# Layer 0's softmax sums taken in 32-column blocks beside the attention heads' sums, and both reciprocals spread over the partitions through DRAM

## The chip, the core and the metric

The kernel runs on one core of a Trainium2 chip. The core has a matrix engine (TensorE, PE in the profile; PEld is its weight load), a vector engine (VectorE, DVE), an activation engine (ScalarE, ACT), a general engine (GpSimd, POOL) and SyncE (SP), which in this kernel only issues DMAs. Each engine works through its own list of instructions in order, and semaphores tie the lists together. The metric is the device time of one execution in microseconds (us), the median of several runs.

## The reference

A graph attention layer and then a masked multi-head attention layer, each with a layer norm and a ReLU ahead of it and a residual sum behind it. `x` is 64 x 256 x 512 in fp32, `adj` is a 256 x 256 mask that all 64 batches share.

```python
# layer 0
h = jnp.maximum(_layernorm(x), 0.0)
Wh = h @ W
logits = leaky_relu((Wh @ a_src)[:, :, None] + (Wh @ a_dst)[:, None, :])     # slope 0.2
attn = softmax(where(adj == 0, -inf, logits), axis=-1)
x = x + attn @ Wh
# layer 1: 8 heads of 64
h = jnp.maximum(_layernorm(x), 0.0)
q, k, v = split_heads(h @ Wq.T + bq), split_heads(h @ Wk.T + bk), split_heads(h @ Wv.T + bv)
attn = softmax(where(adj == 0, -inf, q @ k.T / 8), axis=-1)
x = x + merge_heads(attn @ v) @ Wo.T + bo
```

Two softmax sums are concerned here: in layer 0 one number for each of the 256 nodes of a batch, in layer 1 one for each node and head.

## The kernel before

A group is one batch (`GB = 1`), so there are `G = 64` groups of 256 tokens, in two tiles of 128 partitions. Everything is fp32. Projections and the layer-0 aggregation use a scheme of seven products of half-size blocks instead of eight (`products`, L170, with the sums that it needs made on POOL by `combine`, L163, and the results added up on DVE).

All work is software-pipelined by hand. Each stage is a generator; `first_half` and `second_half` (L1025 to L1031) list, for iteration `i`, which stage makes its next step and for which group: for instance `O` is `(output, -2)`, `E0` is `(weights0, 2)`, `A_OLD` is `(attention, -1)`, `Q0` is `(quarters0, 2)`, `U0` is `(aggregate0, 2)`, `V` is `(project_v, 0)`. The order of these lists is the order of the instructions on every engine. All tiles in PSUM come from one pool of 8 banks (`bank`, L139). Most work tiles in SBUF have a single buffer.

The steps that matter:

- **Layer-0 weights** (`weights0`, L518). ACT makes two exponentials, DVE takes their maximum (L537), POOL applies the mask (L540, `em`) and adds the two halves of the sources (L542, `esum`, 128 x 256). The sum over the 128 partitions is a matmul with a square of ones (L556): its result, `ps`, holds the sum for each of the 256 targets, the same in all 128 partitions. DVE clamps it from below (L558) and takes the reciprocal (L559); the tile is called `rb0` in the code and `rb` in the profile, which leaves numbers out. This is the third step of `E0`, at the end of `first_half`.
- **Layer-0 operands** (`quarters0`, L566), for groups from `PLAIN = 3` on. POOL makes four block sums of `h` (L165 to L168, `hq`), multiplies `em` by the reciprocals (L578), and makes four block differences of it (L588, `eq`). `aggregate0` (L595) then has PE form the seven products (L606, `pu`), which DVE adds up.
- **Head sums** (`head_sums`, L873), inside the last step of `attention`. The sums of a head over the 128 source partitions are taken with a 128 x 32 stationary operand `half`: for each `e` of 4 pairs of heads, the result goes to PSUM partitions 32e to 32e+31, 16 equal rows for each head of the pair (L878, `psm`). DVE takes the reciprocal of that 128 x 256 tile (L886, `rc`).
- **Spreading them** (L905 to L915). To scale the attention output, the reciprocals of a head are needed on all 64 partitions that hold its values. SyncE issues eight DMAs, one per head, each from one row of `rc` to 64 partitions of `rb`. `scale` (L932) multiplies by `rb` on DVE (L936).
- **What follows on POOL.** After `eq`, POOL computes the inverse standard deviations of two layer norms (L474 to L476), on which ACT's normalisations L504 (`h`) and L729 (`xn`) wait; PE transposes `xn` at L750.

For the last two groups the reciprocals are spread by a matmul with `pick` (L922) instead.

Of the kernel before, what the change touches and what calls it, by code (L numbers as in the profile page):

```python
# [9 lines left out]
F32 = mybir.dt.float32  # L10
# [6 lines left out]
P = 128  # L17
# [6 lines left out]
Q = 32  # L24
# [4 lines left out]
def kernel(  # L29
# [26 lines left out]
    nc = tc.nc  # L56
    B, N, D = x.shape
    NC = N // P
    DC = D // P
    NT = GB * NC  # L60
    TOK = NT * P
    G = B // GB
    DH = D // HEADS
# [5 lines left out]
    dram = ctx.enter_context(tc.tile_pool(name="dram", bufs=1, space=bass.MemoryType.DRAM))  # L69
# [12 lines left out]
    ones = const.tile([P, P], F32, tag="ones", name="ones")  # L82
# [49 lines left out]
    def bounded():  # L132
        weights = ctx_b.enter_context(tc.tile_pool(name="weights", bufs=1))
        big = ctx_b.enter_context(tc.tile_pool(name="big", bufs=1))
        work = ctx_b.enter_context(tc.tile_pool(name="work", bufs=1))
# [3 lines left out]
        def bank(shape, name):  # L139
            return ps_mm.tile(shape, F32, tag="mm", name=name)  # L140
# [207 lines left out]
        pick = weights.tile([P, P], F32, tag="pick", name="pick")  # L348
# [10 lines left out]
        def constants():  # L359

            ok = weights.tile([P, 2 * DC + 5], F32, tag="ok", name="ok")
            rows = weights.tile([P, 2 * DC], F32, tag="rows", name="rows")
            gms = []
            for n in range(2):
                w_q = whole((wq_sb, wk_sb)[n])  # L370

                gm = work.tile([P, DC, DH], F32, tag="gram", name=f"gram_{n}", bufs=2)
                gms.append(gm)
                for pair in range(2):
                    pg = bank([P, 2, DH], f"pgram_{n}_{pair}")
                    for e in range(2):
                        for c in range(DC):
                            for r in range(2):
                                at = e * P + r * DH
                                wc = w_q[c // 2][pair][:, c % 2, at : at + DH]  # L380
                                nc.tensor.matmul(
                                    pg[r * DH : (r + 1) * DH, e, :], wc, wc,
                                    start=(c == 0), stop=(c == DC - 1),
                                )
                    yield
                    nc.vector.tensor_copy(gm[:, 2 * pair : 2 * pair + 2, :], pg)
                    yield
            for n, gm in enumerate(gms):
                pgs = [bank([P, DC, DH], f"pgram2_{n}_{r}") for r in range(2)]
                for e in range(DC):  # L390
                    for r in range(2):
                        half_p = slice(r * DH, (r + 1) * DH)
                        part = gm[half_p, e, :]
                        nc.tensor.matmul(pgs[r][half_p, e, :], part, part, start=True, stop=True)
                yield
                for e in range(DC):
                    for r in range(2):
                        half_p = slice(r * DH, (r + 1) * DH)
                        ab = work.tile([P, DH], F32, tag="gabs", name=f"gabs_{n}_{e}_{r}")
                        nc.scalar.activation(  # L400
                            ab[half_p], pgs[r][half_p, e, :], AF.Abs,
                            accum_out=rows[half_p, n * DC + e : n * DC + e + 1],
                        )
                yield
            for _ in range(10):
                yield
            sq = weights.tile([P, 4], F32, tag="sq", name="sq")
            for j, col in enumerate((cols["bq"], cols["bk"])):
                junk = work.tile([P, DC], F32, tag="e2", name=f"junk_c_{j}")
                nc.vector.scalar_tensor_tensor(  # L410
                    junk, col, 1.0, col, op0=ALU.mult, op1=ALU.mult, accum_out=sq[:, j : j + 1]
                )
            for _ in range(4):
                yield
            pq = bank([P, 2], "pq")
            nc.tensor.matmul(pq, ones, sq[:, 0:2], start=True, stop=True)
            yield
            nc.vector.tensor_scalar(
                ok[:, 2 * DC + 2 : 2 * DC + 4], pq, 1.0, None, op0=ALU.is_le
            )  # L420
            yield
            for j in range(2):
                junk = work.tile([P, D], F32, tag="e2", name=f"junk_w_{j}")
                nc.vector.scalar_tensor_tensor(
                    junk, wa[j], 1.0, wa[j], op0=ALU.mult, op1=ALU.mult, accum_out=sq[:, 2 + j : 3 + j]
                )
                yield
            nc.vector.tensor_scalar(ok[:, 0 : 2 * DC], rows, 1.0, None, op0=ALU.is_le)
            nc.vector.tensor_scalar(ok[:, 2 * DC : 2 * DC + 2], sq[:, 2:4], 1.95, None, op0=ALU.is_le)
            yield  # L430
            big_v = weights.tile([P, 1], F32, tag="big_v", name="big_v")
            nc.vector.tensor_reduce(big_v, svs, AX.X, ALU.add)
            nc.vector.tensor_scalar(
                ok[:, 2 * DC + 4 : 2 * DC + 5], big_v, 1.0e6, None, op0=ALU.is_le
            )
            okm = weights.tile([P, 1], F32, tag="okm", name="okm")
            nc.vector.tensor_reduce(okm, ok, AX.X, ALU.min)
            for _ in range(12):
                yield
            pk = bank([1, 1], "pok")  # L440
            nc.tensor.matmul(pk, okm, ones[:, 0:1], start=True, stop=True)
            nc.vector.tensor_scalar(flag, pk, P - 0.5, None, op0=ALU.is_lt)
            yield
            picks()
            yield

        class Stats:

# [30 lines left out]
        nodes, edges, sums0, lefts, norms, qkv, vs, outs = {}, {}, {}, {}, {}, {}, {}, {}  # L479
# [38 lines left out]
        def weights0(g):  # L518
# [22 lines left out]
            esum = work.tile([P, N], F32, tag="esum", name=f"esum_{g}")  # L541
            engine.tensor_tensor(esum, em[:, 0, :], em[:, 1, :], op=ALU.add)  # L542
            edges[g] = [em]
            yield

            if g == 0:
                ps = bank([P, NT], f"ps_{g}")
                for t in range(NT):
                    nc.tensor.matmul(
                        ps[:, t : t + 1], esum[:, t * P : (t + 1) * P], ones[:, 0:1],  # L550
                        start=True, stop=True,
# [7 lines left out]
            nc.vector.reciprocal(rs, rs)  # L559
            edges[g].append(rs)  # L560
            yield


        PLAIN = 3

        def quarters0(g):  # L566

# [257 lines left out]
        def attention(g):  # L825
# [46 lines left out]

            def head_sums():  # L873

                psm = bank([P, N], f"psm_{g}")
                for r in range(2):
                    for e in range(DC):
                        nc.tensor.matmul(  # L878
                            psm[e * Q : (e + 1) * Q, :],
                            half[:, r, :],  # L880
                            sums[e][:, r, :],
                            start=(r == 0),
                            stop=(r == 1),
                        )
                rc = work.tile([P, N], F32, tag="rc", name=f"rc_{g}")
                nc.vector.reciprocal(rc, psm)  # L886
                return rc

            exs = [scores(e) for e in range(DC)]
# [4 lines left out]
            if g == G - 1:  # L894
# [3 lines left out]
                rc = head_sums()  # L898
                values(1, exs[2:4])
            else:  # L900
                for j in range(2):
                    values(j, exs[2 * j : 2 * j + 2])
                rc = head_sums()
            if g < G - 2:
                rb = work.tile([P, DC, N], F32, tag="rb", name=f"rb_{g}")  # L905
                for e in range(DC):
                    for r in range(2):
                        src = rc[e * Q + r * (Q // 2) : e * Q + r * (Q // 2) + 1, :]
                        nc.sync.dma_start(
                            rb[r * DH : (r + 1) * DH, e, :],  # L910
                            bass.AP(
                                tensor=src.tensor, offset=src.offset,
                                ap=[src.ap[0], [0, DH], [1, N]],
                            ),
                        )  # L915
            else:

                yield
                rb = [bank([P, N], f"prb_{g}_{e}") for e in range(DC)]
                for e in range(DC):  # L920
                    rows = slice(e * Q, (e + 1) * Q)
                    nc.tensor.matmul(rb[e], pick[rows, :], rc[rows, :], start=True, stop=True)  # L922
            outs[g] = aT, rb
            yield

# [89 lines left out]
        def aside(n=1):  # L1015
# [3 lines left out]
        K, V, W, O = (project_qk, 0), (project_v, 0), (transform0, 1), (output, -2)  # L1019
        N0, D0, E0, U0 = (normalize0, 3), (normalize0, 2), (weights0, 2), (aggregate0, 2)  # L1020
        Q0 = (quarters0, 2)
# [1 line left out]
        A, A_OLD, BO = (attention, 0), (attention, -1), (bias_rows, 0)  # L1023
        AS, AS_OLD = (scale, -1), (scale, -2)
        first_half = [  # L1025
            (load, 3), O, D0, K, AS_OLD, O, K, O, K, E0, O, K, E0, O, US, A_OLD, K, O, K, BO, O, K, E0,
        ]
        second_half = [
            A_OLD, A, Q0, A, W, N0, W, W, V, N0, W, W, W, N1, W, N1, A, V, V, V, A, N0, N1, U0, V, AS,
            U0, X1, V, X1, V, X1,  # L1030
        ]  # L1031

# [259 lines left out]
```

## Time and profile before

| | |
|---|---|
| time, median of 3 (range) | 2847.4 us (2846.96 to 2849.59) |
| span of the profiled execution | 2845.2 us |
| granted TensorE clock | full speed |
| sum over the partitions for layer 0, L556 | 126 records of 379 ns (median), two for each of 63 matmuls |
| clamp L558, reciprocal L559 (128 x 256) | 411 ns, 1753 ns, 63 of each |
| the same two on 128 x 2 (group 0) | 159 ns, 166 ns |
| head sums L878 | 1024 records of 379 ns; weight load 110 ns |
| reciprocal L886 | 1758 ns, 64 of them |
| broadcast DMAs L909 | 496 of 64 KB, 4.9 us from issue to landing |
| DMA queue q1 | 82470 packets, 107.53 MB, 23.7% of 16 engines |

A duration of a matmul record is that of a pipelined instruction and overlaps the next one's, so what PE spends is read from the starts of successive groups and not from the durations. A "record" is one pass group of an fp32 matmul: each matmul shows two. Lines such as `[1.58 <-PE psm L878]` give the idle time of the engine before the instruction and what ended it.

### The profile page before, as it was taken

To read this page: it belongs to the slowest core of one execution; us is meant where nothing else is said; L and a number is where in the kernel's file an instruction comes from. 1 tells how busy PE (TensorE), PEld (TensorE's weight loads), DVE (VectorE), ACT (ScalarE), POOL (GpSimd) and SP (SyncE) were. 2 spreads that over 40 slices of the span, in tenths; PEclk is the share of its full clock that TensorE was granted. 3 is DMA by queue.
4 is the path that set the end of the run, shared out by engine and by line. 5 is a ranking of instruction groups with operands and counts; after the bars stand their busy time and mean duration, and the time that the engine had idled before them with its cause. 6 is when DMAs were issued, how large, how long until landed. Compare 5 with 4: busy or idle time off the path is not lost. (4 is left out here: it accounts for less than half of the span.)

```text
span 2845.2 us, 53317 instructions
## 1 busy us (share of the span) xinstructions
PE 2828.9 (99%) x20316; PEld 2472.3 (87%) x20316; DVE 2473.5 (87%) x3946; ACT 1257.3 (44%) x3045; POOL 1607.0 (56%) x2016
## 2 busy tenths in 40 slices
PE   9999999999999999999999999999999999999998
PEld 6888988988889889888898898888988988889886
DVE  7998988888889888888898888888988888889875
ACT  5444444443444444434444444344454443444532
POOL 2656556566565565665655655656556556565541
PEclk9999999999999999999999999999999999999999
DMA  4122122221221222212212222122122221221221
GB/s 134 23 38 38 34 42 33 36 45 31 38 38 34 42 33 36 45 31 38 39 33 42 33 36 46 31 38 40 32 42 33 36 45 31 38 42 30 34 42 27
DMA packets 82826, 111.01 MB, mean 39 GB/s; under 512 B 11524, under 2 KB 48644, under 8 KB 82566
## 3 DMA queue, kind: packets, MB, share of 16 engines
q1 hardware_dynamic: 82470, 107.53, 23.7%
q8 instruction: 164, 2.69, 0.4%
q14 instruction: 96, 0.79, 0.1%
q0 software_dynamic: 96, 0.01, 0.0%
HBM read 41.43 MB, written 33.55 MB: 26 GB/s over the span
## 5 line engine op out<-in xcount | busy, mean ns | idle before, releaser
L701 DVE TENSOR_TENSOR x<-po,x 128x1024 f32<-128x1024 f32 x875 | 593.8, 685 | 130.2 <-PE po L207 122.9
L851 DVE TENSOR_TENSOR ex<-ex,maskT 128x512 f32<-128x512 f32 x512 | 435.3, 890 | 0.0
L474 POOL TENSOR_SCALAR ve<-ssq 128x2 f32<-128x2 f32 x127 | 25.1, 198 | 483.8 <-ACT h L463 250.6
L846 ACT ACTIVATE ex<-psc 128x512 f32<-128x512 f32 x512 | 257.7, 627 | 89.5 <-PE psc L838 89.4
L871 ACT COPY aT<-pav 128x512 f32<-128x512 f32 x128 | 74.9, 585 | 499.2 <-PE pav L863 468.1
L511 DVE SCALAR_TENSOR_TENSOR junk<-wa,h 128x512 f32<-128x512 f32 x252 | 276.6, 1098 | 7.9 <-ACT h L504 1.1
L216 PEld LDWEIGHTS pqk<-hs,wq_sb 128*128 128x128 f32 x2016 | 264.4, 192 | 12.9
L216 PE MATMUL pqk<-hs,wk_sb 128*128 128x128 f32 x2016 | 266.3, 275 | 0.0
L216 PE MATMUL pqk<-hs,wq_sb 128*128 128x128 f32 x2016 | 265.8, 275 | 0.0
L207 PE MATMUL pv<-wv_sb,hs 128*128 128x256 f32 x1024 | 262.9, 380 | 0.6 <-DVE v L194 0.5
L540 POOL TENSOR_TENSOR em<-e,maskT 128x512 f32<-128x512 f32 x62 | 79.6, 1283 | 321.7 <-DVE e L537 312.0
L207 PE MATMUL po<-wo_sb,as 128*128 128x256 f32 x992 | 255.2, 380 | 0.0
L207 PE MATMUL po<-w_sb,us 128*128 128x256 f32 x1008 | 248.5, 379 | 0.0
L216 PEld LDWEIGHTS pqk<-hs,wk_sb 128*128 128x128 f32 x2016 | 245.4, 192 | 0.0
L838 PE MATMUL psc<-qk 64*128 64x256 f32 x2048 | 239.0, 383 | 0.3 <-DVE rc L886 0.3
L863 PE MATMUL pav<-ex,v 128*64 128x256 f32 x2048 | 235.4, 382 | 0.0
L838 PEld LDWEIGHTS psc<-qk 64*128 64x128 f32 x2048 | 193.1, 187 | 46.9 <-issue 25.0
L165 POOL TENSOR_TENSOR hs<-hT 128x256 f32<-128x256 f32 x64 | 47.0, 735 | 319.2 <-PE pv L207 319.2
L853 DVE TENSOR_TENSOR sm<-ex 128x512 f32<-128x512 f32 x256 | 210.5, 822 | 8.9
L863 PEld LDWEIGHTS pav<-ex,v 128*64 128x64 f32 x2048 | 141.2, 137 | 85.8 <-issue 20.3
L207 PEld LDWEIGHTS po<-w_sb,us 128*128 128x128 f32 x1008 | 191.4, 190 | 26.3 <-DVE x L701 0.3
L216 PEld LDWEIGHTS pqk<-hT,wq_sb 128*128 128x128 f32 x1512 | 198.2, 192 | 9.6
(211 smaller groups left out, 6564.5 us busy)
## 6 DMA issues: line engine op xcount, KB each, us to landing
x<-in_x_dram SPq DMA_DIRECT2D x64, 512.0 KB, 5.6
out_dram<-x SPq DMA_DIRECT2D x128, 256.0 KB, 2.0
rb<-rc SPq DMA_DIRECT2D x496, 64.0 KB, 4.9
wq_sb<-in_L_gnn_Wq_dram SPq DMA_DIRECT2D x4, 256.0 KB, 8.4
wk_sb<-in_L_gnn_Wk_dram SPq DMA_DIRECT2D x4, 256.0 KB, 6.7
w_sb<-in_L_gnn_W_dram SPq DMA_DIRECT2D x4, 256.0 KB, 6.6
wv_sb<-in_L_gnn_Wv_dram SPq DMA_DIRECT2D x4, 256.0 KB, 6.6
wo_sb<-in_L_gnn_Wo_dram SPq DMA_DIRECT2D x4, 256.0 KB, 6.0
```

What stands on the lines that cost most here:

```text
L165: nc.gpsimd.tensor_tensor(s[:, 0], a(1, 0), a(1, 1), op=ALU.add)
L207: nc.tensor.matmul(dst[:, 0:HD], left[:, c, :], wt[:, slot, c, :], start=c == 0, stop=c == 1)
L216: nc.tensor.matmul(dst[:, at : at + P], wt[:, slot, c, e * P : (e + 1) * P], left[:, c, :], start=c == 0, stop=c == 1,)
L511: nc.vector.scalar_tensor_tensor(junk, (wa if g else pas)[a], 1.0, h[:, t, :], op0=ALU.mult, op1=ALU.mult, accum_out=dst[:, t : t + 1],)
L540: engine.tensor_tensor(em, e1, maskT, op=ALU.mult)
L701: nc.vector.tensor_add(dst, src, dst)
L838: nc.tensor.matmul(psc[r][:, m, :], qk[rows, 2 + e % 2, m * P : (m + 1) * P], qk[rows, e % 2, :], start=True, stop=True,)
L846: nc.scalar.activation(ex[:, r, :, :], psc[r], AF.Exp, scale=SCALE)
L851: nc.vector.tensor_mul(ex[:, r, :, :], ex[:, r, :, :], maskT)
L853: nc.vector.tensor_add(sm, ex[:, :, 0, :], ex[:, :, 1, :])
L863: nc.tensor.matmul(pav[r * DH : (r + 1) * DH, i, :], v[j][:, m, at : at + DH], pair[i][:, r, m, :], start=(m == 0), stop=(m == NC - 1),)
L871: nc.scalar.copy(aT[j], pav)
```

## The change

For groups from 3 on, the layer-0 sum leaves `weights0`, and is taken in `head_sums` of the group three behind. `esum` is cut in four pieces of 64 targets; each is multiplied by a 128 x 32 block of ones, and its result goes to PSUM partitions 32e to 32e+31, in 64 more columns of the tile of the head sums. So the clamp and the reciprocal run on 64 columns instead of 256. As the reciprocals then lie in four blocks of partitions, they are written to DRAM (128 x 64) and read back spread over all 128 partitions (`rb0`). The heads' reciprocals take the same way: one write of 128 x 256 and two reads, in place of eight broadcasts from SBUF. The third step of `E0` goes, and in `second_half` one step of `V` moves ahead of the first `U0`. Some small tiles share tags. The purpose is to take work from PE and DVE, and a bank of PSUM.

```diff
@@ weights0
             edges[g] = [em]
-            yield
+            if g >= PLAIN:
+                edges[g].append(esum)
+            yield
+            if g >= PLAIN:
+                return
@@ head_sums
-                psm = bank([P, N], f"psm_{g}")
+                psm = bank([P, N + DH], f"psm_{g}")
+                rc = work.tile([P, N + DH], F32, tag="rc", name=f"rc_{g}")
+                g0 = g + PLAIN
+                if g0 < G:
+                    part = slice(N, N + DH)
+                    for e in range(DC):
+                        rows = slice(e * Q, (e + 1) * Q)
+                        nc.tensor.matmul(
+                            psm[rows, part], ones[:, 0:Q], edges[g0][1][:, e * DH : (e + 1) * DH],
+                            start=True, stop=True,
+                        )
                 for r in range(2):
                     for e in range(DC):
                         nc.tensor.matmul(
-                            psm[e * Q : (e + 1) * Q, :],
+                            psm[e * Q : (e + 1) * Q, 0:N],
 ...
-                rc = work.tile([P, N], F32, tag="rc", name=f"rc_{g}")
-                nc.vector.reciprocal(rc, psm)
+                if g0 < G:
+                    nc.vector.tensor_scalar_max(rc[:, part], psm[:, part], 1e-38)
+                    nc.vector.reciprocal(rc[:, part], rc[:, part])
+                    rows_d = dram.tile([P, DH], F32, tag="rows0_d", name=f"rows0_d_{g0}", bufs=2)
+                    nc.sync.dma_start(rows_d, rc[:, part])
+                    rb0 = work.tile([P, N], F32, tag="rb0", name=f"rb0_{g0}")
+                    nc.sync.dma_start(
+                        rb0.rearrange("p (e n) -> p e n", e=DC),
+                        bass.AP(
+                            tensor=rows_d.tensor, offset=rows_d.offset,
+                            ap=[[0, P], [Q * DH, DC], [1, DH]],
+                        ),
+                    )
+                    edges[g0][1] = rb0
+                nc.vector.reciprocal(rc[:, 0:N], psm[:, 0:N])
@@ attention, last step
-                for e in range(DC):
-                    for r in range(2):
-                        src = rc[e * Q + r * (Q // 2) : e * Q + r * (Q // 2) + 1, :]
-                        nc.sync.dma_start(
-                            rb[r * DH : (r + 1) * DH, e, :],
-                            bass.AP(
-                                tensor=src.tensor, offset=src.offset,
-                                ap=[src.ap[0], [0, DH], [1, N]],
-                            ),
-                        )
+                rows_d = dram.tile([P, N], F32, tag="rows_d", name=f"rows_d_{g}", bufs=2)
+                nc.sync.dma_start(rows_d, rc[:, 0:N])
+                for r in range(2):
+                    nc.sync.dma_start(
+                        rb[r * DH : (r + 1) * DH, :, :],
+                        bass.AP(
+                            tensor=rows_d.tensor, offset=rows_d.offset + r * (Q // 2) * N,
+                            ap=[[0, DH], [Q * N, DC], [1, N]],
+                        ),
+                    )
@@ order of the stages
-            (load, 3), O, D0, K, AS_OLD, O, K, O, K, E0, O, K, E0, O, US, A_OLD, K, O, K, BO, O, K, E0,
+            (load, 3), O, D0, K, AS_OLD, O, K, O, K, E0, O, K, E0, O, US, A_OLD, K, O, K, BO, O, K,
-            A_OLD, A, Q0, A, W, N0, W, W, V, N0, W, W, W, N1, W, N1, A, V, V, V, A, N0, N1, U0, V, AS,
+            A_OLD, A, Q0, A, W, N0, W, W, V, N0, W, W, W, N1, W, N1, A, V, V, V, A, N0, N1, V, U0, AS,
             U0, X1, V, X1, V, X1,
```

More of the change, by code (lines that the diff above doesn't have):

```diff
@@ L398, in constants @@
                         half_p = slice(r * DH, (r + 1) * DH)
-                        ab = work.tile([P, DH], F32, tag="gabs", name=f"gabs_{n}_{e}_{r}")
+                        ab = work.tile([P, DH], F32, tag="rc", name=f"gabs_{n}_{e}_{r}")
                         nc.scalar.activation(
@@ L445, in constants @@
             yield
+        PLAIN = 3
         class Stats:
@@ L561, in weights0 @@
             yield
-        PLAIN = 3
         def quarters0(g):
@@ L921, in attention @@
                     rows = slice(e * Q, (e + 1) * Q)
-                    nc.tensor.matmul(rb[e], pick[rows, :], rc[rows, :], start=True, stop=True)
+                    nc.tensor.matmul(rb[e], pick[rows, :], rc[rows, 0:N], start=True, stop=True)
             outs[g] = aT, rb
```

## The prediction

> **What bounds the kernel now.** I read the busy shares first, then the waits, then one period of each engine's timeline. The busy shares say TensorE (PE):
>
> ```profile
> PE 2828.9 (99%) x20316; PEld 2472.3 (87%) x20316; DVE 2473.5 (87%) x3946; ACT 1257.3 (44%) x3045; POOL 1607.0 (56%) x2016
> ```
>
> A pipelined PE can look busy while it stalls, so I asked who PE waits for. In the whole span the waits of PE matmuls add up to about 11 us, nearly all of it at the start. The timeline then shows the period: the layer-0 mask product on POOL starts at the same point of two successive groups.
>
> ```profile
> 1398.98 1.27 POOL L540 TENSOR_TENSOR em<-e,maskT 128x512 f32<-128x512 f32 x1 [5.08 <-DVE e L537]
> ...
> 1442.73 1.27 POOL L540 TENSOR_TENSOR em<-e,maskT 128x512 f32<-128x512 f32 x1 [5.08 <-DVE e L537]
> ```
>
> One batch takes 43.75 us. Here is the PE stretch that the change rewrites (start, duration, line, output<-input, records):
>
> ```profile
> 1404.47 1.06 PE L216 MATMUL pqk<-hs,wk_sb 128*128 128x128 f32 x8
> 1405.37 0.60 PE L556 MATMUL ps<-esum,ones 128*128 128x256 f32 x2
> 1405.89 3.67 PE L863 MATMUL pav<-ex,v 128*64 128x256 f32 x32
> 1409.50 1.07 PE L878 MATMUL psm<-sm,half 128*32 128x256 f32 x16
> 1410.50 3.73 PE L838 MATMUL psc<-qk 64*128 64x256 f32 x32
> 1414.15 1.13 PE L207 MATMUL po<-w_sb,uT 128*128 128x256 f32 x4
> ...
> 1423.75 0.61 PE L606 MATMUL pu<-em,h 128*128 128x128 f32 x4
> ```
>
> Every start follows the previous group's end: PE is the bound in every stretch, so what counts is the PE time taken out per batch, provided that nothing new makes PE wait. Each fp32 matmul is two records. The full-width projections of 4 records at 1421.16, 1422.03 and 1422.89 follow each other by 0.865 us, so a 256-column record costs 0.216 us; the 8 records of 128 columns at 1404.47 take 0.90, so one costs 0.112. The head sums run their 16 records in 1.00 us, not in 16 x 0.216 = 3.46: four 32-column strips of the array work at once (4 x 0.216 = 0.865, and 0.135 for entering the group).
>
> The other engines around it, for the steps below:
>
> ```profile
> 1406.86 0.41 DVE L558 TENSOR_SCALAR rb<-ps 128x256 f32<-128x256 f32 x1
> 1407.30 1.75 DVE L559 RECIPROCAL rb<-rb 128x256 f32<-128x256 f32 x1
> 1410.64 1.76 DVE L886 RECIPROCAL rc<-psm 128x256 f32<-128x256 f32 x1 [1.58 <-PE psm L878]
> ```
>
> ```profile
> 1410.60 0.72 POOL L168 TENSOR_TENSOR hq<-h,hq 128x256 f32<-128x256 f32 x1
> 1411.28 1.41 POOL L578 TENSOR_TENSOR em<-em,rb 128x256 f32<-128x256 f32 x2
> ...
> 1415.24 0.46 POOL L588 TENSOR_TENSOR eq<-em,eq 128x128 f32<-128x128 f32 x1
> 1419.78 0.19 POOL L474 TENSOR_SCALAR ve<-ssq 128x2 f32<-128x2 f32 x1 [4.09 <-ACT h L463]
> ```
>
> ```profile
> 1423.89 1.50 ACT L504 ACTIVATE h<-x,nmr,rstd 128x512 f32<-128x512 f32 x2
> 1425.59 1.52 ACT L729 ACTIVATE xn<-x,nmr,rstd 128x512 f32<-128x512 f32 x2 [0.19 <-POOL nmr L476]
> ```
>
> ```profile
> x<-in_x_dram SPq DMA_DIRECT2D x64, 512.0 KB, 5.6
> out_dram<-x SPq DMA_DIRECT2D x128, 256.0 KB, 2.0
> rb<-rc SPq DMA_DIRECT2D x496, 64.0 KB, 4.9
> ```
>
> DVE sits idle 1.58 us before the head sums' reciprocal; POOL has the layer-0 operands (eq) ready at 1415.70, 8 us before PE reads them at 1423.75.
>
> **What the Trainium skill says.** "TensorE: Matmul & The Clock Gate", Part 3, says that outputs at PSUM partitions 32j land in separate column strips and run concurrently; the head sums above agree (1.00 us for 3.46 us of records). "TensorEngine Tiling (Array Packing)", Key Properties, says that changing the tiling mode drains the array; the trace agrees in size: the two records of L556 need 0.43 and the next group starts 0.52 after, so the switch costs about 0.09. "DMA: Bandwidth & Descriptors", Anatomy of one DMA, puts the fixed cost of a DMA (on the GpSimd path) at about 2.0 us, mostly the write receipt; the 256 KB stores here, from SyncE's queue, land in 2.0 us in all.
>
> **The change, part by part.** t is time from the start of the head-sum group (1409.50 in the kernel before).
>
> 1. The full-width layer-0 sum goes, for groups 3 to 63, 61 of them. It costs PE 2 x 0.216 = 0.43 us; the 0.09 of the switch stays, since the projections now go straight over to the half-width values. Saved: 0.43.
> 2. Four 32-column matmuls of 64 moving columns come, inside the head-sum group, already in the four-strip mode, so no new switch. Halving the columns halves a record (0.216 to 0.112), so 64 columns should cost about 0.057. All four strips at once: 2 x 0.057 = 0.11 us. Not shown before are such short records; the trace bounds them by 0.11 each if the weight load sets the pace (a 32-column load takes 0.110 there), which makes 0.22, and by 8 x 0.057 = 0.46 if the strips don't overlap. I take 0.12, since the head sums' own records do overlap. Net: 0.31 per group.
> 3. DVE: clamp and reciprocal shrink from 256 to 64 columns. The trace also has them on 2 columns (0.159 and 0.166) and on 256 (0.411 and 1.753); between, 64 columns cost 0.22 and 0.55. DVE loses 2.16 - 0.77 = 1.39 us per group, 85 us in all. It is worth nothing at the end, because PE doesn't wait for DVE. But the 0.77 now stands between the head sums and their reciprocal, so that ends at t = 1.14 + 0.12 + 0.77 + 1.76 = 3.8, not 2.9. Queued behind it are a mask product and the adds of transform0 (L701), which had 0.36, 0.84, 0.17 and 0.44 us of idle time before them; the lag of under 1 us is taken up there. The bank of the head sums is next wanted by the second layer-0 output product at about t = 5.7.
> 4. The layer-0 reciprocals now reach POOL by DRAM. Clamp and reciprocal are done at t = 1.26 + 0.77 = 2.05 (both wait for the whole head-sum tile). The 32 KB write lands 1.5 to 2.0 us after issue (stores: 2.0): t = 3.9. SyncE's queue holds everything behind until then; only the other write, two reads and the next x load stand there, and x is loaded three batches ahead. The read back is 512 packets of 256 B, 32 for each of 16 engines. Start and receipt cost 1.3 (a store's 2.0 less its 8 packets per engine of 0.087, from the packet records); at 0.03 to 0.131 us a packet (the latter the mean of queue q1: 23.7% of 16 engines over 82470 packets) it is 2.3 to 5.5; I take 3.2. rb0 lands at t = 7.1 (6.2 to 9.4).
> 5. POOL waits for it, some 5 us, after hq. Behind: the two em products (1.37) and four eq differences (3.05), done at t = 11.5; PE wants the first at 14.25 + 0.12 + 0.86 = 15.2 (one value product now stands ahead of it). Then the three rstd/nmr operations (1.26), at t = 12.8; ACT reads nmr at 1423.89, t = 14.4. So rb0 may come as late as 8.7 with no engine noticing, and 0.6 later still before the transposes on PE at 1427.74 miss xn (done 1427.11). Cost: nothing.
> 6. The heads' reciprocals: one write and two reads for eight broadcasts, issued after part 4, landing at about t = 10 to 12; DVE reads them at 1429.29, t = 19.8. Nothing. Moving the third E0 step, the value product and the reuse of tags reorder work with slack: nothing.
>
> Sum: 61 x 0.31 = 18.9 us; 2847.4 - 18.9 = 2828.5.
>
> **The rivals.** (a) Weight loads pace the short records: 0.43 - 0.22 = 0.21 per group, 13 us, 2834.5. For: the load's 0.110 exceeds 0.057. Against: loads of different strips overlap in the head sums. (b) The strips don't overlap: 0.43 - 0.46, no gain, 2849. Against: the head sums. (c) The DRAM trip is late and PE waits: slower. If each of the two DMAs took the 4.9 us of a broadcast, rb0 lands at t = 11.9, nmr at 17.6, ACT 3.2 late, the transposes 2.6 late after their 0.6 of slack: 2828.5 + 61 x 2.6 = 2987. For: POOL works in order and has statistics behind. Against: broadcasts read one partition many times and queue in eights; a store needs 2.0.
>
> **How the numbers follow.** My forecast 0.74, (a) 0.14, (b) 0.03, (c) 0.06, some unseen gain on a third engine 0.03 (below 2825). The time is the forecast's, 2828.5. The range 2825 to 2837 takes in the forecast with parts 2 and 4 at their bounds, and (a); it leaves out (b), (c). Faster: 0.74 + 0.14 + 0.03 and a little of (c), 0.92; same 0.03; slower 0.05.
>
> **What would show it.** Right: a period of 43.44; L556's successor left with 4 records; the new matmuls start together and the head-sum group takes 1.12; DVE busy near 2389, its idle time before the clamp about 3.3; POOL waiting about 5 us a group for the DMA of rb0, and PE waiting for neither POOL nor ACT. Wrong: a period above 43.6, a head-sum group of 1.4 us, or PE waits on xn, em or eq.

## The result and the profile after

| | before | after |
|---|---|---|
| time, median of 4 runs each (range) | 2848.07 us (2846.96 to 2849.59) | 3052.49 us (3050.78 to 3061.94) |
| ratio, with its 95% interval | | 1.0724 (1.0701 to 1.0747) |
| mean granted TensorE clock | 1.0 | 0.974 |

The kernel became 204 us slower; the forecast was 19 us faster. The busy shares of the page after, to be held against the line of before:

```profile
PE 2890.9 (95%) x20682; PEld 2523.6 (83%) x20682; DVE 2384.5 (78%) x3946; ACT 1262.6 (41%) x3045; POOL 1651.8 (54%) x2016
```

DVE lost its 89 us (2473.5 to 2384.5). PE is busy for longer than before although work was taken from it, and it now leaves 5% of the span idle. The waits tell why (waiting engine and line, what released it, us in total, times, longest):

```profile
POOL em L583 <- DMA rb<-rows_d: 532.7, 61, 11.8
...
ACT h L507 <- POOL nmr L479: 172.1, 48, 5.4
...
PEld pt L755 <- ACT uT L622: 147.9, 47, 3.8
...
PE pt L755 <- ACT uT L622: 139.0, 47, 3.7
```

Read from top to bottom, this is one chain: POOL waits for the DRAM read back in all 61 groups, 8.7 us on average; ACT then waits for the statistics that stand behind it on POOL; PE waits for ACT. But there are 61 waits at the top and only 47 at the bottom. From one head-sum group to the next (starts of the first record of L888), the distance is 43.42 us in one group of four (but for one of these 15, at 44.43) and 48.4 us on average in the other three (median 48.3, most between 47.2 and 49.8): 45 late groups at 4.98 us. The 60 distances exceed 60 x 43.42 by 225 us, which is the whole loss against the forecast.

The same stretch of PE's timeline in a late group (start, duration, line, output<-input; in brackets the idle time before and what ended it):

```profile
1367.47 0.32 PE L888 MATMUL psm<-esum,ones 128*32 128x64 f32 x8
1367.61 1.05 PE L894 MATMUL psm<-sm,half 128*32 128x256 f32 x16
1368.59 3.72 PE L843 MATMUL psc<-qk 64*128 64x256 f32 x32
...
1382.71 0.61 PE L611 MATMUL pu<-em,h 128*128 128x128 f32 x4
...
1385.38 0.61 PE L611 MATMUL pu<-em,hq 128*128 128x128 f32 x4
1388.85 1.12 PE L755 MATMUL pt<-ident,xn 128*128 128x128 f32 x4 [2.85 <-ACT uT L622]
1389.76 1.92 PE L207 MATMUL pv<-wv_sb,hT 128*128 128x256 f32 x4
1391.46 0.95 PE L755 MATMUL pt<-ident,xn 128*128 128x128 f32 x4
```

The new layer-0 matmuls move the next group's start by 0.14 us (1367.47 to 1367.61), and both together take 1.12. Up to L611, nothing waits. Then PE stands still for 2.85 us. And after it, the four records of `pt` take 0.91 us from start to start (1388.85 to 1389.76), and four records of `pv` 1.70 instead of 0.865. The windows say why (stretch, its length, busy us and instructions of PE, PEld, DVE, ACT, POOL, then PEclk, DMA share, GB/s):

```profile
1386.00:1388.80 2.80, 0.00 (x0) 0.00 (x0) 0.56 (x2) 2.54 (x5) 0.88 (x2) 0.99 0.66 215
1388.80:1391.40 2.60, 2.55 (x8) 2.15 (x9) 2.44 (x6) 0.00 (x0) 0.00 (x0) 0.50 0.00 0
1391.40:1395.00 3.60, 3.60 (x23) 3.33 (x22) 2.84 (x7) 1.19 (x2) 1.49 (x3) 0.89 0.00 0
```

After the pause the granted clock is 0.50. In between stands ACT, in order: `h` waits for POOL's statistics, `xn` follows, and `uT`, the copy whose end releases PE, stands behind both:

```profile
1385.25 1.52 ACT L507 ACTIVATE h<-x,nmr,rstd 128x512 f32<-128x512 f32 x2 [3.17 <-POOL nmr L479]
1387.02 1.52 ACT L734 ACTIVATE xn<-x,nmr,rstd 128x512 f32<-128x512 f32 x2 [0.25 <-POOL nmr L479]
1388.44 0.35 ACT L622 COPY uT<-pu 128x256 f32<-128x256 f32 x1
```

So a late group loses twice: the wait itself (139.0 us over the run), and PE work at half clock, which shows up as 81 us more "busy" than the same 20682 records take at full clock (2809.7 in `e8_both_packed` below). 139 + 81 = 220 of the 225 us. The mean clock says the same: 0.026 of 3050 us is 79.

POOL in the same group:

```profile
1369.02 0.73 POOL L168 TENSOR_TENSOR hq<-h,hq 128x256 f32<-128x256 f32 x1
1379.04 1.42 POOL L583 TENSOR_TENSOR em<-em,rb 128x256 f32<-128x256 f32 x2 [9.30 <-DMA rb<-rows_d]
...
1383.55 0.19 POOL L477 TENSOR_SCALAR ve<-ssq 128x2 f32<-128x2 f32 x1
...
1386.79 0.19 POOL L479 TENSOR_TENSOR nmr<-nmean,rstd 128x2 f32<-128x2 f32 x1
```

and SyncE's queue, where the length is that of the issue alone:

```profile
1369.57 0.33 SPq L906 DMA_DIRECT2D rows_d<-rc  x1
1371.05 0.38 SPq L908 DMA_DIRECT2D rb<-rows_d  x1
1371.47 0.50 SPq L937 DMA_DIRECT2D rows_d<-rc  x1
1379.34 1.25 SPq L939 DMA_DIRECT2D rb<-rows_d  x2
```

The reciprocals are ready at 1369.5 and the read is issued at 1371.05, when the write has landed. Then nothing happens for 8 us, to the read's end just before 1379.04. The write of the heads' reciprocals, issued at 1371.47, comes through only then too:

```profile
rows_d<-rc SPq DMA_DIRECT2D x62, 128.0 KB, 8.0
...
rows_d<-rc SPq DMA_DIRECT2D x61, 32.0 KB, 1.4
```

So 32 KB land in 1.4 us, and 128 KB need 8.0, behind the read. The Trainium skill, "DMA: Bandwidth & Descriptors", Queues, rings and completion order, says that each DMA engine consumes its descriptors in the order of the ring; a write behind a slow read in the same queue fits that. In `e3_heads_only`, with no read ahead of it, the same write takes 1.7.

In the packet records of the trace the read's first packet comes 1.05 us after its issue and the last one 7.1 to 8.9 us after it in the late groups (median 7.7), 4.3 to 5.2 us in the early ones (median 4.5). So its 512 packets of 256 B take 6.6 or 3.5 us: one packet per engine each 0.206 us in the late groups. A single record is only 0.015 us long: a busy share made from records does not see this. The two windows below are a late and an early group during the read; POOL waits in both, and the DMA engines show a share of 0.10 and 0.15, as if they had nothing to do:

```profile
1372.00:1378.00 6.00, 6.00 (x31) 5.10 (x28) 4.46 (x7) 4.76 (x13) 0.00 (x0) 1.00 0.10 29
1469.00:1472.00 3.00, 3.00 (x16) 2.64 (x15) 2.52 (x3) 1.97 (x7) 0.00 (x0) 1.00 0.15 42
```

What repeats every four groups? By its offset in the kernel's DRAM area, as the program lays it out, the tile of each group (32 KB) lies 160 KB behind that of the last one, so its place repeats every four groups modulo 128 KB. In the early groups it starts 112 KB past a multiple of 128 KB, and the four rows that the read uses (8 KB apart) lie two on each side of the next multiple; in the late groups all four lie on one side.

**Theories.** T1: the read is slow because all 128 partitions read the same four pieces of 256 B (`ap=[[0, P], [Q * DH, DC], [1, DH]]`: a step of 0 over the partitions). Rivals: the read is slow for its 512 small packets or its bytes; the heads' DMAs in the same queue hold it up; the loss lies in the order on PE or in the heads' part, and the POOL wait is harmless. A second question was how a wait on POOL becomes 5 us on PE.

### The profile page after: what moved, and what is told of

Same layout as the page of the kernel before. It is cut to its first block, busy times and chain, and to the rows that moved or that the text cites. A ratio compares the mean times of both kernels' runs of the same rounds, so it can differ in the third digit from the quotient of the medians.

```text
span 3049.7 us, 53855 instructions
## 1 busy us (share of the span) xinstructions
PE 2890.9 (95%) x20682; PEld 2523.6 (83%) x20682; DVE 2384.5 (78%) x3946; ACT 1262.6 (41%) x3045; POOL 1651.8 (54%) x2016
## 5 line engine op out<-in xcount | busy, mean ns | idle before, releaser
L583 POOL TENSOR_TENSOR em<-em,rb 128x256 f32<-128x256 f32 x122 | 102.2, 858 | 532.7 <-DMA rb<-rows_d 532.7
L514 DVE SCALAR_TENSOR_TENSOR junk<-wa,h 128x512 f32<-128x512 f32 x252 | 264.2, 1048 | 7.9 <-ACT h L507 1.1
L207 PE MATMUL pv<-wv_sb,hs 128*128 128x256 f32 x1024 | 269.5, 399 | 0.6 <-DVE v L194 0.5
L755 PE MATMUL pt<-ident,xn 128*128 128x128 f32 x512 | 105.0, 342 | 143.9 <-ACT uT L622 139.0
L207 PE MATMUL pv<-wv_sb,hT 128*128 128x256 f32 x768 | 225.8, 422 | 0.0
L207 PEld LDWEIGHTS pv<-wv_sb,hs 128*128 128x128 f32 x1024 | 201.9, 203 | 26.9 <-DVE v L194 0.9
L755 PEld LDWEIGHTS pt<-ident,xn 128*128 128x128 f32 x512 | 79.7, 178 | 166.9 <-ACT uT L622 147.9
```

Source lines behind the costliest of these rows:

```text
L207: nc.tensor.matmul(dst[:, 0:HD], left[:, c, :], wt[:, slot, c, :], start=c == 0, stop=c == 1)
L514: nc.vector.scalar_tensor_tensor(junk, (wa if g else pas)[a], 1.0, h[:, t, :], op0=ALU.mult, op1=ALU.mult, accum_out=dst[:, t : t + 1],)
L583: nc.gpsimd.tensor_tensor(em[:, m, :], em[:, m, :], rb, op=ALU.mult)
L755: nc.tensor.transpose(pt[:, c, :], xn[:, t, c * P : (c + 1) * P], ident)
```

## The experiments

Each kernel is the changed one with the edit shown, but for `e3_heads_only`; `before` stood at 2847.7 to 2847.9 us beside them. Where no interval is given, the time is of one run. The effects are 15 to 200 us, and the kernel before spread over 3 us.

**1. Is it the wait of POOL?** `e1_const` multiplies by another tile, so POOL waits for no DMA; all DMAs stay. It leaves out the normalisation of the layer-0 softmax.

```diff
-nc.gpsimd.tensor_tensor(em[:, m, :], em[:, m, :], rb, op=ALU.mult)
+nc.gpsimd.tensor_tensor(em[:, m, :], em[:, m, :], maskT[:, 0, :], op=ALU.mult)
```

> The changed kernel, but POOL multiplies the layer-0 weights by a constant tile that is there from the start instead of by the reciprocals from DRAM; all DMAs stay. Left out: the layer-0 softmax is not normalised. Theory L (POOL waits for rb0, and everything queued behind it on POOL is late): no wait on POOL, every group at the 43.42 us that one group in four has in the changed kernel, 2828 us in all (2825 to 2832). Rival S (the new order of stages, or the heads' reciprocals by DRAM, is what stalls PE): the time stays near 3050.

2859.32 us: 193 us come back. The wait is the cause of nearly all of the loss. 31 us remain above 2828, which I had not expected; the waits of this kernel:

```profile
DVE aT L966 <- DMA rb<-rows_d: 57.0, 41, 3.8
...
PE po L207 <- DVE aT L966: 21.8, 24, 3.0
```

The slow read still holds up the heads' write (7.6 us) and the reads behind it, and now the scaling that needs them is late on DVE. In the changed kernel itself the trace shows no such wait of DVE for these reads: its late groups are 5 us longer.

**2. Which half of the change?** `e2_l0_only` keeps the layer-0 trip and spreads the heads by the old eight broadcasts; `e3_heads_only` is the kernel before with only the heads' trip through DRAM. The core of the edits (the lines are those of the diff above, taken the one way or the other):

```diff
 e2_l0_only
-rows_d = dram.tile([P, N], F32, tag="rows_d", name=f"rows_d_{g}", bufs=2)
...
+for e in range(DC):
+    for r in range(2):
+        src = rc[e * Q + r * (Q // 2) : e * Q + r * (Q // 2) + 1, 0:N]
...
 e3_heads_only (against the kernel before)
-for e in range(DC):
...
+rows_d = dram.tile([P, N], F32, tag="rows_d", name=f"rows_d_{g}", bufs=2)
+nc.sync.dma_start(rows_d, rc)
...
```

> The layer-0 part of the change alone: the heads' reciprocals are spread by eight broadcasts from SBUF, as before the change. Theory L: the wait on POOL stays, 3030 to 3060 us, rb0 landing 7 to 8 us after its issue in three groups of four. If the heads' own DRAM trip were to blame (by filling the DMA engines, or by SyncE's queue), the time would fall to about 2830.

> The heads' part alone: the kernel before with one DRAM write and two reads in place of the eight broadcasts. Theory L: nothing waits for them (DVE needs them some 19 us after the head sums), so 2847 us, within 0.2% of before, period 43.75 us. Rival S: slower, above 2900.

3048.5 and 2846.8 us (before beside them: 2847.85). The layer-0 trip alone makes the whole loss, and with the old broadcasts behind it the read takes about as long as in the changed kernel: first packet 1.05 us after its issue, last 7.0 to 8.5 (median 7.5), and 4.1 to 5.1 in every fourth group. Its line in part 6 of the page:

```profile
rb<-rows_d SPq DMA_DIRECT2D x61, 128.0 KB, 7.8
```

So the heads' DMAs are not what holds it up. The heads' trip alone costs and brings nothing.

**3. Same pieces, or many packets?** Two kernels, both with the read in four DMAs of 32 partitions each, alike in packets, bytes, issues and written data. They differ in one number: in `e4_hot4` all partitions still read the same four rows, in `e5_spread4` partition p of each DMA reads row p of each block (the 32 rows of a block are equal, so the values are the same).

```diff
-ap=[[0, P], [Q * DH, DC], [1, DH]],          one DMA
+ap=[[0, Q], [Q * DH, DC], [1, DH]],          e4_hot4, four DMAs
+ap=[[DH, Q], [Q * DH, DC], [1, DH]],         e5_spread4, four DMAs
```

> Control for the next study: the read back of the layer-0 reciprocals cut into four DMAs of 32 partitions each, same 512 packets of 256 B from the same four 256 B pieces of DRAM. Same packets, so under every theory about as slow as the changed kernel or slower by the three more issues (about 1.1 us a group): 3040 to 3110 us.

> As the control with four DMAs, but partition p of each 32 reads row p of its block in DRAM, where the same 64 reciprocals stand in all 32 rows: the same 512 packets of 256 B, from 128 different pieces instead of 4. Theory H (reads of the same few bytes of DRAM are served one after another, some 80 packets a microsecond): the read back takes 2 to 4 us instead of 6 to 8, all groups at 43.42 us, 2828 us (2825 to 2836). Rival C (many small packets are slow wherever they read): as the control, 3053 us.

3053.14 and 2827.63 us. The read's line in part 6 of the page, first `e4_hot4`:

```profile
rb<-rows_d SPq DMA_DIRECT2D x244, 32.0 KB, 4.5
```

and `e5_spread4`:

```profile
rb<-rows_d SPq DMA_DIRECT2D x244, 32.0 KB, 1.8
```

On POOL, in `e4_hot4` and then in `e5_spread4`:

```profile
1379.02 1.41 POOL L583 TENSOR_TENSOR em<-em,rb 128x256 f32<-128x256 f32 x2 [9.11 <-DMA rb<-rows_d]
```

```profile
1363.79 1.41 POOL L583 TENSOR_TENSOR em<-em,rb 128x256 f32<-128x256 f32 x2 [5.25 <-DMA rb<-rows_d]
```

T1 stands: with the same 512 packets, the last one comes 2.9 us after the first issue (median, in the fourth groups as in the others), where `e4_hot4` takes 7.4 us in its late groups, and all groups past the start have the distance 43.42. POOL still waits 307.8 us in `e5_spread4`, and the kernel runs at the forecast: the wait of 5 us that the prediction allowed is free, that of 9 is not.

**4. Per byte or per packet, and does it suffice to pack?** In `e6_row1` and `e7_rows32` the write puts the four blocks side by side, so that one row of 1 KB holds all 256 reciprocals, and 128 packets of 1 KB do. In `e6_row1` all partitions read row 0; in `e7_rows32` 32 different rows, four times each.

```diff
-nc.sync.dma_start(rows_d, rc[:, part])
+nc.sync.dma_start(bass.AP(..., ap=[[DH, DC], [N, Q], [1, DH]]), rc[:, part])
-ap=[[0, P], [Q * DH, DC], [1, DH]],
+ap=[[0, P], [1, N]],                         e6_row1
+ap=[[N, Q], [0, P // Q], [1, N]],            e7_rows32
```

> The write puts the four blocks side by side (32 rows of 256 reciprocals, all equal), and all 128 partitions read the first row: 128 packets of 1 KB instead of 512 of 256 B, but still from one spot of 1 KB. Theory H, if the spot is slow by bytes: the same 128 KB from the same four 256 B pieces, as slow as the changed kernel, 3030 to 3060 us. Rival C (slow by packets): 128 packets at 80 a microsecond take 1.6 us, 2828 us.

> The same write, and partition p reads row p // 4: 128 packets of 1 KB from 32 different rows. Under H and under C the read back is short (2 to 3 us after its issue) and POOL's wait goes from some 9 us to 4 or 5: every group at 43.42 us, 2828 us (2825 to 2836). If DRAM itself were too far (write, receipt and read each some microseconds whatever is read), it would stay above 2900 us.

2827.76 us, and 2827.66 (median of 4; ratio to before 0.9925, 0.991 to 0.994). From the start of the first packet to the end of the last: 1.04 us from one row, 0.54 from 32 rows. POOL in `e6_row1` and then in `e7_rows32`:

```profile
1363.63 1.42 POOL L583 TENSOR_TENSOR em<-em,rb 128x256 f32<-128x256 f32 x2 [4.87 <-DMA rb<-rows_d]
```

```profile
1363.24 1.42 POOL L583 TENSOR_TENSOR em<-em,rb 128x256 f32<-128x256 f32 x2 [4.43 <-DMA rb<-rows_d]
```

So even packed, the packets of one row take twice as long as those of many rows; but the price goes by the packet rather than by the byte: for the same 128 KB, 128 packets from one row take 8.1 ns each, and 512 from four rows took 13 ns each.

**5. Does the place in DRAM matter?** Still 512 packets of 256 B from four pieces, but the pieces lie 128 KB apart. To keep the write small, only the four rows that are read are written.

```diff
+wide = [dram.tile([DC, WIDE], F32, tag=f"wide{n}", name=f"wide{n}") for n in range(2)]   # WIDE = 32768
-rows_d = dram.tile([P, DH], F32, tag="rows0_d", name=f"rows0_d_{g0}", bufs=2)
-nc.sync.dma_start(rows_d, rc[:, part])
+rows_d = wide[g0 % 2]
+nc.sync.dma_start(rows_d[:, 0:DH], rc[0:P:Q, part])
-ap=[[0, P], [Q * DH, DC], [1, DH]],
+ap=[[0, P], [WIDE, DC], [1, DH]],
```

> The changed kernel, but only one row of each block is written, and the four rows lie 128 KB apart in DRAM instead of 8 KB; the read is the same 512 packets of 256 B from four pieces. The groups that are quick in the changed kernel are those whose four pieces lie on both sides of a 128 KB boundary. If that is what makes them quick, all groups are now at least as quick: the read's last packet 2.8 to 4.5 us after issue, 2828 us (2825 to 2840). If the place in DRAM has nothing to do with it: 3050 us.

2828.99 us; the last packet comes 2.7 to 3.5 us after issue (median 2.9), with no difference between the fourth groups and the others, and every group past the start has 43.42. POOL:

```profile
1364.56 1.41 POOL L585 TENSOR_TENSOR em<-em,rb 128x256 f32<-128x256 f32 x2 [4.62 <-DMA rb<-wide]
```

First to last: 1.8 us in the median, against 6.6 with the pieces in one stretch of 128 KB and 3.5 with a boundary between them. That is 78, 147 and 284 packets per us for one, two and four stretches: the rate goes with the number of stretches, which fits the one early group in four. (The place is not the only thing that changed: the write is smaller, though it had landed before the read was issued, and two areas are used in turn where the changed kernel has a new tile for each group.)

**6. What turns a late `em` into 5 us?** Two candidates stood behind the wait on POOL: the layer-0 operands themselves (`eq`), which PE wants at L611, and the statistics of the layer norms. `e9_split` puts a step between the block sums and the multiplication by `rb0`, and moves the latter behind the first `N0` statistics.

```diff
                 combine(a, s)
+                yield
                 for m in range(NC):
...
-A_OLD, A, Q0, A, W, N0, W, W, V, N0, W,
+A_OLD, A, Q0, A, W, N0, W, W, V, N0, Q0, W,
```

> The changed kernel with its slow read back, but POOL's part of quarters0 cut in two: the block sums hq stay in their place, the products with rb0 and the differences eq come after the first of the two rstd/nmr groups. Theory L says that PE stalls because the statistics stand behind POOL's wait for rb0: with the first group of them ahead, ACT's h is on time, only xn is late, by about a microsecond in three groups of four: 2840 to 2900 us. If PE stalled for em or eq themselves, nothing would be gained: 3050 us.

2937.16 us, clock 0.997: half of the loss is gone, though I expected more. The waits of PE in this kernel:

```profile
PE pt L756 <- ACT uT L623: 84.1, 61, 2.2
...
PE pu L612 <- POOL eq L594: 3.7, 6, 1.5
```

L612 hardly waits for `eq`, even though the multiplication is as late as ever: the operands themselves were hardly the issue (in the changed kernel, too, PE waits for `eq` only 4.0 us in all). `pt` still waits, now in all 61 groups, for 1.4 us each: the multiplication starts 9.9 us or more after the start of the reciprocal in every group (median 10.1), and the second set of statistics, which stays behind it, is late even where the read is early. So what the wait delays is the statistics; moving one of the two sets ahead takes the longest waits away and puts a short one in every group. The half clock is nearly gone: by the clock records of the trace, none of the 56 pauses of up to 1.8 us is followed by it, and all five of 2.23 us, the longest, are, at once or within 0.8 us.

**7. How much of it is the clock?** `e11_busy` gives PE 25 transposes without a use after the last layer-0 product, just where it stood still.

```diff
+if slot == B22:
+    for _ in range(25):
+        nc.tensor.transpose(dst[:, HD : HD + P], ident, ident)
```

> The changed kernel with 25 transposes of the identity (2.8 us of PE at full clock, their result unused) behind the last layer-0 product, in the place where PE stands idle in the late groups. If the late groups lose 2.8 us by the wait and another 1.5 to 2 us because PE runs at half clock after standing idle, the filler hides in the wait and gives the second part back: late groups about 46.5 us instead of 48.2, early ones some 2 us longer than 43.42, about 3000 us in all (2980 to 3020). If the clock is not what costs, the late groups stay at 48 and the early ones grow: about 3080 us.

3021.99 us, clock 0.999, just above the expected span. The pause is filled (PE timeline):

```profile
1372.71 2.89 PE L617 MATMUL pu<-ident 128*128 128x128 f32 x25
1375.44 0.60 PE L758 MATMUL pt<-ident,xn 128*128 128x128 f32 x4
```

`pt` runs at full speed again, and no group shows the half clock. Early groups now take 46.15 us, 2.73 more, late ones 46.6 in the median instead of 48.3. The kernel does 2.73 us of useless work in every group and is still 30 us faster than the changed one: the clock's share of the loss is real, nearly 2 us of 5 in a late group. POOL's wait is unchanged (526.1 us).

The changed kernel alone says the same. The clock records of its trace show the half clock in 38 of the 45 late groups, in stretches of 3.41 or 6.83 us whose starts all lie on one grid of 3.413 us, wherever the pause falls. In the seven others it does not come, after pauses of the same length (3.1 us on average, 3.0 in the 38), and they take 47.1 us on average instead of 48.6.

**8. Is DRAM needed at all?** `e12_sbuf4` drops the layer-0 trip and broadcasts each of four 64-column rows straight from SBUF to 128 partitions.

```diff
-rows_d = dram.tile([P, DH], F32, tag="rows0_d", name=f"rows0_d_{g0}", bufs=2)
-nc.sync.dma_start(rows_d, rc[:, part])
+for e in range(DC):
+    src = rc[e * Q : e * Q + 1, part]
+    nc.sync.dma_start(rb0[:, e * DH : (e + 1) * DH],
+        bass.AP(..., ap=[src.ap[0], [0, P], [1, DH]]))
```

> The layer-0 reciprocals not by DRAM but by four broadcasts from SBUF, one row of each block to all 128 partitions (128 packets of 256 B each). The eight broadcasts before the change took 10.9 us from the first issue to the last landing; half as many, with a quarter of the bytes in each packet but the same number of packets, should take 4 to 6 us: rb0 in time, 2828 us (2825 to 2845). If broadcasts from one partition are as slow by packets as reads from one spot of DRAM: above 2950 us.

2828.14 us, every group 43.42. POOL:

```profile
1365.15 1.41 POOL L583 TENSOR_TENSOR em<-em,rb 128x256 f32<-128x256 f32 x2 [6.36 <-DMA rb<-rc]
```

No write comes first, but reading one row 128 times is slow here too: the last packet comes 6.0 us after the first issue. The multiplication starts 7.1 us after the start of the reciprocal (median). The latest start that was still free in any kernel here was 7.89 (`e4_hot4`), and one of 8.41 cost 1.0 us (the group of 44.43 in the changed kernel), so this version has about 0.8 us to spare.

**9. The best of it.** `e8_both_packed` is `e7_rows32` with the heads' trip packed in the same way: rows of 4 KB, read from 16 different ones.

```diff
-nc.sync.dma_start(rows_d, rc[:, 0:N])
+nc.sync.dma_start(bass.AP(..., ap=[[N, DC], [DC * N, Q], [1, N]]), rc[:, 0:N])
-ap=[[0, DH], [Q * N, DC], [1, N]],
+ap=[[DC * N, Q // 2], [0, 2 * DH // Q], [1, DC * N]],
```

> As the study before, and the heads' reciprocals the same way: written so that each of 32 rows in DRAM holds the four pairs of heads side by side, and read as 64 packets of 4 KB from 16 different rows, twice. If the heads' reads are off the path once the layer-0 read is short, no difference from the study before: 2828 us (2825 to 2834), 0.7% faster than before the change. If they still bind in some groups, this one is faster than the study before by up to 20 us.

2827.59 us (median of 5; ratio to before 0.9927, 0.9914 to 0.9941): faster than before by 0.7%, and the same as `e7_rows32`. Its busy shares and its `pt`:

```profile
PE 2809.7 (99%) x20682; PEld 2468.3 (87%) x20682; DVE 2340.6 (83%) x3946; ACT 1257.8 (45%) x3045; POOL 1564.4 (55%) x2016
```

```profile
1374.68 0.60 PE L755 MATMUL pt<-ident,xn 128*128 128x128 f32 x4
```

PE is back at 99%, and no pause stands before `pt`. The heads' reads land in 3.8 us instead of 6.5, which is worth nothing, since nobody waits for them once the layer-0 read is quick.

## Why the prediction was wrong, step by step

- **Steps 1 and 2, the PE work, were right.** The four short matmuls cost 0.14 us (0.12 forecast), the head-sum group takes 1.12 (1.12), and where nothing waits, the distance is 43.42 (43.44). Rivals (a) and (b) are out. The forecast time itself, 2828.5, is met within 1 us by six kernels that differ from the changed one in nothing but how the reciprocals travel (2827.59 to 2828.99).
- **Step 3 was right.** DVE is busy for 2384.5 us (2389), and idle 3.38 us before the clamp (3.3):

```profile
1368.72 0.23 DVE L903 TENSOR_SCALAR rc<-psm 128x64 f32<-128x64 f32 x1 [3.38 <-PE psm L894]
1368.98 0.55 DVE L904 RECIPROCAL rc<-rc 128x64 f32<-128x64 f32 x1
```

- **Step 4 failed, in one term: the price of a packet in the read back.** The write was over-priced, if anything (1.4 us; 1.5 to 2.0 forecast). The read took 7.9 us where 3.2 was taken and 5.5 was the upper bound. The upper price, 0.131 us, was the mean duration of the records of all packets of the queue, down to those of 4 bytes, and the lower one, 0.03, had no line beside it. Here it was 0.206 us per packet and engine, and the prediction's own sum with that price, 1.3 + 32 x 0.206, gives the measured 7.9. The reason is that the step of 0 sends 512 packets to the same four pieces (experiment 3). Hence `rb0` at t = 11.6 and not 7.1. The diff shows that zero plainly, and the trace before had a nearer relative: the eight broadcasts, also 512 packets out of a few rows, there of SBUF, took 9.5 us from the first packet to the end of the last, 0.30 us per packet and engine (issued over 6.0 us). The prediction set them aside because they "read one partition many times"; the read back does the same with four pieces of DRAM.
- **Step 5 had the right slack and the wrong verdict.** It let `rb0` come as late as t = 8.7, or 9.3 with the transposes' reserve. Measured: starts of the multiplication of up to 7.89 us after L904's start, which is t = 9.4, cost nothing, and 8.41 cost 1.0 us. The upper bound of step 4 itself, 9.4, lay past both limits of the prediction, so "Cost: nothing" did not hold for its whole range. It fell with step 4, and for the reason that the step named: the statistics behind the wait.
- **Step 6 was wrong without a price.** The heads' reciprocals were to land at t = 10 to 12; their write hangs behind the slow read (8.0 us), their reads are issued at t = 11.9 only and the second lands at t = 20.4 (in the group shown), just past the 19.8 at which DVE wants them. DVE waits for them in `e1_const` alone.
- **Rival (c), at 0.06, was what happened.** Its sizes for a late group were good: `rb0` at 11.9 (measured 11.6), ACT 3.2 late (3.17 in the group shown), PE 2.6 late (2.85 there). The first of them was luck: 4.9 us for each of the two DMAs, where the write took 1.4 and the read 7.9. It missed two things. One group in four is early, so 46 groups pay and not 61; and a pause of 3 us is paid again, in part, as half clock, some 1.8 us per late group. 61 x 2.6 = 159 was forecast, 139 + 81 came. Its argument against itself, "a store needs 2.0", spoke of a write, not of a read of one place.

What stays open: which part of the memory serves a stretch of 128 KB, and why a hot piece is slow there. The runs show that the read's time depends on how many different pieces, and in how many such stretches, the packets hit; not the mechanism.

## What to carry to other kernels

Before a broadcast is routed through DRAM, look at the read's address pattern: a step of 0 over the partitions makes every packet hit the same few bytes, and then neither the bytes nor the records' own durations price it. If the data already lie in several equal rows, let each partition read another one, and pack the pieces into one long row (here 6.6 us became 0.5). And where a wait is put on an engine that works in order, list everything queued behind it and compare the slack with the slowest plausible transfer, not with the likeliest: on PE, a stall of 3 us was paid again in clock here, with some 1.8 us.

## What the runs showed of the hardware that I had not expected

- Reads of 256 B out of four hot pieces: 78 packets per us with the pieces 8 KB apart in one stretch of 128 KB, 147 with a multiple of 128 KB between them, 284 with all four 128 KB apart. One hot row of 1 KB: 123 packets per us; 32 rows: 237.
- A slow read holds up a write queued behind it on the same queue: 8.0 us instead of 1.7.
- PE at half clock after a pause of 2.85 us, for 3.41 us; in `e9_split`, after all five pauses of 2.23 us and after none of up to 1.8. The Trainium skill, "TensorE: Matmul & The Clock Gate", Part 1, puts the half rate after at least one idle window of some 3.4 us; the half rate agrees (0.50), but here pauses from 2.2 us on were enough, and not always: it came with 38 of the 45 pauses of 2.4 to 3.7 us in the changed kernel. It came in steps of 3.41 us on one grid; in some groups the first transposes still ran at full speed and the half clock followed a little later.
